# The order of the last products of a dense layer, and where its output blocks are joined to the rows

## The chip, the core and the metric

The kernel runs on one core of a Trainium2 chip. The time is device microseconds of one execution, given as the median of three runs; the profile comes from an execution of its own. Engines are named PE (TensorE, matrix products; PEld is its weight load), DVE (VectorE), ACT (ScalarE), POOL (GpSimd) and SP (SyncE, which issues DMAs). ACT can issue DMAs too.

## What is computed

A graph of 1250 nodes with 512 features and 20,000 edges passes two layers. The first is a normed neighbour mean, a linear map and kernel attention. The second is this one:

```python
h = relu(layernorm(x))
agg = segment_sum(h[src], dst, num_segments=N)
h = (1.0 + eps) * h + agg
h = relu(batch_norm(h @ W1 + b1, g1, be1))     # 512 -> 1024
h = h @ W2 + b2                                # 1024 -> 512: the second dense layer
h = relu(batch_norm(h, g2, be2))
return x + h
```

`batch_norm` takes mean and variance of each feature over all 1250 nodes, so no output of a feature can be finished before every node's sum for it is there. Adding a constant such as `b2` to a feature moves its mean and leaves its variance.

## The kernel before

**Layout.** Activations are kept transposed: features on the 128 partitions, nodes along the free dimension, padded to 1252 = 2 x 626 (`HN`). The output of the second dense layer, `o`, has four blocks f = 0 to 3 of 128 features. `xs` holds the residual rows, nodes on partitions, in ten row groups (nine of 128, the last of 98).

**Seven products.** Both dense layers use a Strassen-Winograd scheme: the weights and the activations are quartered, and seven products of quarters (numbered 1 to 7) with sums before and after take the place of eight. Class `Dense` (L749) does this for two output blocks at a time. Instance `a` has blocks 0 and 2, `b` blocks 1 and 3 (block m + 2 i). `multiply(p)` (L758) issues product p on PE into two banks of PSUM, one for each half (313 nodes, `NH`) of 626: 2 halves x 4 steps over the contraction, each an f32 matmul that the profile shows as two records, so 16 records. Products 2, 3 and 5 go to banks B, the others to banks A. Products 1, 6, 7, 4 follow each other in A without clearing it, 5 and 3 in B.

**After a product** (`after`, L792): ACT copies A aside with the bias added (`keep`, after 1, 6, 7). DVE adds such a copy to B and so writes a quarter of `o` (`join`, after 2, 7, 3), then takes statistics of the two halves (`stats`). After product 4, ACT writes the quarter (block i = 1, first 626 nodes) straight from A with the bias. With `direct`, used for the very last product, DVE takes the statistics from A in PSUM rather than from `o`, and adds the bias to the means in them (L812).

**Norm and rows.** `norm` (L816) calls `affine` (L123): aggregate four sets of statistics (`bn_aggr`), root on ACT, reciprocal and three small operations on DVE, giving `sb`, a scale and a shift for each feature. `apply` (L870) norms a block of `o` in place: nodes 0 to 511 and 1024 to 1249 on DVE, 512 to 1023 on ACT. `rows_of` (L878) turns the block back to rows with ten 128 x 128 transposes on PE into three PSUM tiles; `finish` (L886) adds max(., 0) to `xs` on DVE (two operations of 4 row groups, one of 1 group and one of 98 rows) and issues four output DMAs (256, 256, 64 and 49 KB), two on SP and two on ACT.

**Order.** The loop at L921 gives the order of the last products of `a` and `b`: a6, a5, b6, a7, b5, b7, a4 (norm of block 2), a3 (norm of block 0, then the rows of block 2), b3 (norm of block 1, then the rows of block 0), and then b4 with the statistics taken directly (L930). The rows of block 1 are transposed behind b4 and joined only among the joins of block 3 (L932 to L940). Matmuls and transposes keep the program's order on PE, and so do the marked DVE operations (`order`); each engine works in order, waiting on semaphores of the others. All eight PSUM banks belong to one pool (`mm`): four to `a`, four to `b`; a new tile takes the place of the oldest when its last reader is done.

Of the kernel before, what the change touches and what calls it, by code (L numbers as in the profile page):

```python
# [11 lines left out]
F32 = mybir.dt.float32  # L12
# [4 lines left out]
AF = mybir.ActivationFunctionType  # L17
ALU = mybir.AluOpType
# [3 lines left out]
N, D, E = 1250, 512, 20000  # L22
HID = 2 * D
KD = D // 128
KH = HID // 128
# [4 lines left out]
BSPLIT = [(0, 512), (512, 512), (1024, 226)]  # L30
# [7 lines left out]
S = 128  # L38
NJ = -(-N // S)
ROWS = [min(S, N - j * S) for j in range(NJ)]  # L40
# [14 lines left out]
HN = 626  # L55
NH = HN // 2
# [13 lines left out]
def sorted_graph(ctx: ExitStack, tc: tile.TileContext, ed, x, n1g, n1b, n2g, n2b, wconv, bconv,  # L70
                 wq, wk, wv, wo, proj, eps, w1, b1, g1, be1, w2, b2, g2, be2, out):
    nc = tc.nc
# [50 lines left out]
    def affine(sb, st, g, b, shift=None):  # L123


        mv = tmp.tile([128, 2], F32, name="mv")
        r = tmp.tile([128, 2], F32, name="r")
        nc.vector.bn_aggr(mv, st.rearrange("p i s -> p (i s)"))  # L128
        nc.scalar.activation(r[:, 0:1], mv[:, 1:2], AF.Sqrt, bias=epsc, scale=1.0)  # L129
        if shift is not None:  # L130
            nc.vector.tensor_tensor(mv[:, 0:1], mv[:, 0:1], shift, ALU.add)
        nc.vector.reciprocal(r[:, 0:1], r[:, 0:1])
        nc.vector.tensor_tensor(r[:, 1:2], r[:, 0:1], negT[:, g:g + 1], ALU.mult)
        nc.vector.tensor_tensor(sb[:, 0:1], r[:, 0:1], vT[:, g:g + 1], ALU.mult)
        nc.vector.scalar_tensor_tensor(sb[:, 1:2], mv[:, 0:1], r[:, 1:2], vT[:, b:b + 1], op0=ALU.mult, op1=ALU.add)
# [15 lines left out]
    mm = att.enter_context(tc.tile_pool(name="mm", bufs=4, space=PSUM))  # L151
# [27 lines left out]
    col, at, r = {}, {}, 0  # L179
    for name, v in vectors.items():  # L180
        k = v.shape[0] // 128
# [329 lines left out]
    for f in range(KD):  # L511
        ps = mm.tile([128, TOK], F32, name="mm")
# [18 lines left out]
    mm = ctx.enter_context(tc.tile_pool(name="mm2", bufs=8, space=PSUM, reuse_waits="tile"))  # L531
# [3 lines left out]
    xs = p2.tile([S, NJ, D], F32, name="xs")  # L535
# [29 lines left out]
    for f in range(KD):  # L565
        fs = slice(f * 128, (f + 1) * 128)
        st = tmp.tile([128, 3, 6], F32, name="st")
        for i, (n0, n) in enumerate(BSPLIT if f == KD - 1 else ESPLIT):
            c = slice(n0, n0 + n)
            ps = banks.pop(0)[:, :n] if banks else mm.tile([128, n], F32, name="mm")  # L570
# [9 lines left out]
            b = at["bconv"] + f  # L580
# [8 lines left out]
        sb = tmp.tile([128, 2], F32, name="sb")  # L589
# [86 lines left out]
    for g, after in zip(groups[2:], groups[3:] + ((),)):  # L676
        w = slice(g[0], g[-1] + 1)
        order(nc.vector.reciprocal(rs[:, w], rs[:, w]))
        order(nc.vector.scalar_tensor_tensor(nb[:, w], mv[:, w, 0], -1.0, rs[:, w], op0=ALU.mult, op1=ALU.mult))
        for j in g:  # L680
            n = ROWS[j]

            for t in (hi, h2):
                nc.scalar.activation(t[:n, j, :], xs[:n, j, :], AF.Relu, bias=nb[:n, j:j + 1], scale=rs[:n, j:j + 1])
        for j in after:
            joined(j)
            measured(j)
        if after:
            root(after)
        for j in g:  # L690
            lows(j)
# [24 lines left out]
    for t in range(6, NJ):  # L716
# [8 lines left out]
        for j in range(3 * (t - 6), min(3 * (t - 6) + 3, NJ)):  # L725
            n = ROWS[j]
# [14 lines left out]
    def add(engine, out, x, y, op):  # L741
        order(engine.tensor_tensor(out, x, y, op))
# [6 lines left out]
    class Dense:  # L749
# [42 lines left out]
        def after(self, p, direct=False):  # L792

            if p == 1:
                self.keep(1, 0)
            elif p == 2:
                self.join(0, 0, 1)
            elif p == 6:
                self.keep(6, 0)
            elif p == 7:  # L800
                self.keep(7, 1)
                self.join(1, 1, 7)
            elif p == 3:
                self.join(0, 1, 6)
            elif p == 4:
                for c in range(2):
                    o, b, st, _ = self.part(1, 0, c)
                    nc.scalar.activation(o, self.A[c], AF.Identity, bias=b, scale=1.0)
                    if direct:

                        order(nc.vector.bn_stats(st, self.A[c]))
                        order(nc.vector.tensor_scalar(st[:, 1::3], st[:, 1::3], b, None, op0=ALU.add))  # L812
                if not direct:
                    self.stats(1, 0)

        def norm(self, i, g, be):  # L816
            sb = tmp.tile([128, 2], F32, name="sb4", bufs=4)
            f = self.m + i * self.half
            affine(sb, self.st[i], at[g] + f, at[be] + f)
            return f, sb  # L820

    w2t = weight(w2, "w2", p4, "w2")
# [17 lines left out]
    for m0 in (0, 2):  # L840
        d = {c: Dense(ops1, m, KH // 2, hid, "b1") for c, m in zip("ab", (m0, m0 + 1))}
        for p, c in ((1, "a"), (2, "a"), (1, "b"), (2, "b"), (6, "a"), (6, "b"), (5, "a"), (5, "b"), (7, "a"), (7, "b"),
# [15 lines left out]
            if p == 3:  # L858
                relu(d[c], 0)
                k = d[c].m  # L860
# [9 lines left out]
    def apply(o, sb):  # L870
        for i, (n0, n) in enumerate(BSPLIT):
            c = o[:, n0:n0 + n]
            if i == 1:
                nc.scalar.activation(c, c, AF.Identity, bias=sb[:, 1:2], scale=sb[:, 0:1])
            else:
                order(nc.vector.tensor_scalar(c, c, sb[:, 0:1], sb[:, 1:2], op0=ALU.mult, op1=ALU.add))

    def rows_of(o):  # L878
        for n0, n in BSPLIT:
            j0 = n0 // S  # L880
            ps = mm.tile([S, 4, 128], F32, name="mm")
            for j in range(j0, -(-(n0 + n) // S)):
                nc.tensor.transpose(ps[:ROWS[j], j - j0, :], o[:, j * S:j * S + ROWS[j]], ident)
            yield ps

    def finish(f, sets):  # L886

        fs = slice(f * 128, (f + 1) * 128)
        for i, ((n0, n), ps) in enumerate(zip(BSPLIT, sets)):
            j0 = n0 // S  # L890
            js = range(j0, -(-(n0 + n) // S))
            whole = [j for j in js if ROWS[j] == S]
            w = slice(j0, j0 + len(whole))
            order(nc.vector.scalar_tensor_tensor(xs[:, w, fs], ps[:, :len(whole), :], 0.0, xs[:, w, fs],  # L894
                                                 op0=ALU.max, op1=ALU.add))
            queue = nc.scalar if i == 1 else nc.sync
            queue.dma_start(out[j0 * S:(j0 + len(whole)) * S, fs].rearrange("(j p) d -> p j d", p=S), xs[:, w, fs])
            for j in js:
                if j not in whole:
                    k = ROWS[j]  # L900
                    order(nc.vector.scalar_tensor_tensor(xs[:k, j, fs], ps[:k, j - j0, :], 0.0, xs[:k, j, fs],
                                                         op0=ALU.max, op1=ALU.add))
                    nc.scalar.dma_start(out[j * S:j * S + k, fs], xs[:k, j, fs])
            yield
# [13 lines left out]

    for k in range(KH // 2):
        add(nc.vector, rh[0, 1][:, k, :], rh[0, 1][:, k, :], th[:, 0, k, :], ALU.subtract)  # L920
    for d, p in ((a, 6), (a, 5), (b, 6), (a, 7), (b, 5), (b, 7), (a, 4), (a, 3), (b, 3)):  # L921
        d.multiply(p)
        d.after(p)
        if p in (3, 4):
            f, sb = d.norm(p - 3, "g2", "be2")
            apply(o[:, f], sb)
        if p == 3:
            for _ in finish(2 * (d is a), rows_of(o[:, 2 * (d is a)])):
                pass
# [12 lines left out]

@with_exitstack
# [455 lines left out]
def tile_gnn(ctx: ExitStack, tc: tile.TileContext, x, src, dst, *rest):  # L1399
# [171 lines left out]
    with tc.If(v == 0) as arms:  # L1571
        sorted_graph(tc, ed, x, *rest)
# [33 lines left out]
```

## Time and profile before

| | |
|---|---|
| time, median of 3 runs | 376.24 us (375.83 to 377.05) |
| profiled execution, its own time | 377.66 us |
| its span, first to last instruction | 375.9 us |
| PE busy | 357.0 us (95%) |
| DVE, ACT, POOL busy | 235.6, 157.4, 35.4 us |
| granted TensorE clock, mean | 0.989 |
| DMA moved | 18.06 MB |

The span is shorter than the execution's own time, because something precedes the first and follows the last instruction. Times in the profile are us from the start of the span. A timeline line gives start, duration, engine, line of the kernel, operation, what it writes and reads with shapes, how often it comes (merged neighbours), and in brackets how long the engine had been idle and who ended that. In the two lines of slices each digit is a fortieth of the span in tenths. A line of a stretch gives its bounds, length, busy time of PE, PEld, DVE, ACT and POOL with the number of instructions, the granted clock, the mean busy share of the 16 DMA engines and GB/s. A line of a source line's instructions gives how many there were, their least, median and longest duration in ns, and the first and last start.

### The profile page before, as it was taken

The page shows a single profiled execution, that of the slowest core. Times are in us where ns is not written, and L with a number is a line of the kernel's source. Part 1 is how long each engine was busy: PE and PEld are TensorE (multiplying, and loading weights), DVE is VectorE, ACT ScalarE, POOL GpSimd, SP SyncE. Part 2 cuts the span into 40 slices and gives each one's busy share as a digit, 9 for nine tenths or more (in the row PEclk, how much of TensorE's full clock was granted, in tenths as well). Part 3 has the DMA queues.
Part 4 walks back from the last instruction along what each step waited for, and adds up shares of the span by engine and source line. Part 5 has one row for each costly group of instructions (what it writes and reads, how often), then busy time and mean ns, then how long its engine had stood idle before and what let it go on. Part 6 is the DMA issues. An engine that isn't in the chain of part 4 may idle for free.

```text
span 375.9 us, 4922 instructions
## 1 busy us (share of the span) xinstructions
PE 357.0 (95%) x1840; PEld 263.3 (70%) x1840; DVE 235.6 (63%) x585; ACT 157.4 (42%) x310; POOL 35.4 (9%) x55
## 2 busy tenths in 40 slices
PE   8799989999999999999999999999999999999970
PEld 4665555676566699998768888777777777777750
DVE  6899994649897235687887232182780888212783
ACT  5498549727565360111157312232652542111230
POOL 3000000000000005000000009610062000000000
PEclk9999999999999999999999999999999999999995
DMA  6943020000000471000000000240000000000045
GB/s 200 289 166 128 16 98 0 2 1 2 0 1 2 151 279 67 0 3 0 0 2 0 2 0 1 55 171 0 2 0 1 1 2 0 1 0 2 10 126 144
DMA packets 13285, 18.06 MB, mean 48 GB/s; under 512 B 1341, under 2 KB 6658, under 8 KB 13254
## 3 DMA queue, kind: packets, MB, share of 16 engines
q1 hardware_dynamic: 10622, 16.41, 13.0%
q10 hardware_dynamic: 2632, 1.27, 1.3%
q8 instruction: 16, 0.26, 0.3%
q14 instruction: 15, 0.12, 0.1%
HBM read 15.11 MB, written 2.56 MB: 47 GB/s over the span
## 4 chain that ended last, share of the span: by engine, by line
PE 83%; DVE 11%; ACT 2%; issue 1%; DMA 1%; DVEq 0%
PE mm L764 29%; PE mm L707 12%; PE mm L575 12%; PE hw L422 10%; PE mm L245 3%; PE mm L449 2%; PE mm L521 2%; PE mm L482 2%; PE sc L267 2%; PE acc L217 2%; DVE op L206 1%; DVE xs L894 1%; PE mm L226 1%; PE mm L701 1%; DVE kmx L334 1%; PE mm L472 1%
## 5 line engine op out<-in xcount | busy, mean ns | idle before, releaser
L779 ACT ACTIVATE kept<-mm,vT 128x313 f32<-128x313 f32 x36 | 18.5, 521 | 49.6 <-PE mm L764 48.5
L422 PE MATMUL hw<-wconv,xn 128*128 128x512 f32 (+1 forms) x80 | 37.1, 605 | 0.3 <-ACT adj L220 0.3
L707 PE MATMUL mm<-hi,adj 128*128 128x512 f32 (+2 forms) x100 | 32.2, 400 | 0.5 <-DVE hi L655 0.4
L707 PE MATMUL mm<-lo,adj 128*128 128x512 f32 (+2 forms) x100 | 31.7, 395 | 0.0
L129 ACT ACTIVATE r<-mv,epsc 128x1 f32<-128x1 f32 x16 | 4.7, 292 | 52.1 <-DVE mv L128 52.1
L764 PE MATMUL mm<-hid,w 128*128 128x313 f32 x96 | 25.8, 427 | 0.0
L422 PEld LDWEIGHTS hw<-wconv,xn 128*128 128x128 f32 (+1 forms) x80 | 14.1, 188 | 16.4 <-issue 14.8
L575 PE MATMUL mm<-adj,lo 128*128 128x416 f32 (+3 forms) x120 | 25.1, 355 | 0.0
L575 PE MATMUL mm<-adj,hi 128*128 128x416 f32 (+3 forms) x120 | 25.1, 355 | 0.0
L206 DVE TENSOR_TENSOR op<-iop,prow 128x1280 f16<-128x1280 f16 (+2 forms) x27 | 20.8, 769 | 6.0 <-PE acc L217 5.6
L784 DVE TENSOR_TENSOR hid<-mm,kept 128x313 f32<-128x313 f32 x24 | 10.9, 477 | 20.4 <-ACT kept L779 16.9
L764 PEld LDWEIGHTS mm<-hid,w 128*128 128x128 f32 x96 | 18.2, 190 | 6.9
L575 PEld LDWEIGHTS mm<-adj,hi 128*128 128x128 f32 x120 | 21.9, 189 | 1.1
L575 PEld LDWEIGHTS mm<-adj,lo 128*128 128x128 f32 x120 | 21.8, 189 | 1.0
L707 PEld LDWEIGHTS mm<-hi,adj 128*128 128x128 f32 (+2 forms) x100 | 18.4, 186 | 5.8 <-DVE hi L655 1.4
L698 DVE SCALAR_TENSOR_TENSOR z<-h,e,mm 128x512 f32<-128x512 f32 (+1 forms) x10 | 7.0, 745 | 23.5 <-PE mm L707 15.7
L707 PEld LDWEIGHTS mm<-lo,adj 128*128 128x128 f32 (+2 forms) x100 | 18.5, 186 | 4.6 <-DVE lo L648 0.2
L217 PEld LDWEIGHTS <-op 128*128 128x128 f16 x250 | 13.7, 97 | 9.1 <-issue 4.7
L217 PE MATMUL acc<-ok,op 128*128 128x100 f16 x250 | 16.2, 208 | 3.4 <-DVE ok L206 2.7
L784 DVE TENSOR_TENSOR o<-mm,kept 128x313 f32<-128x313 f32 x12 | 5.7, 482 | 21.5 <-ACT kept L779 20.8
L702 ACT COPY zT<-mm 128x512 f32<-128x512 f32 (+1 forms) x10 | 5.3, 583 | 29.3 <-PE mm L701 29.3
L764 PE MATMUL mm<-tz,w 128*128 128x313 f32 x64 | 17.5, 426 | 0.0
(249 smaller groups left out, 717.0 us busy)
## 6 DMA issues: line engine op xcount, KB each, us to landing
w<-in_L_gnn_W_dram SPq DMA_DIRECT2D x2, 2048.0 KB
xs<-in_x_dram SPq DMA_DIRECT2D x1, 2304.0 KB
wk<-in_L_gnn_Wk_dram SPq DMA_DIRECT2D x1, 1024.0 KB
x<-in_x_dram SPq DMA_DIRECT2D x1, 1024.0 KB
v<-in_L_gnn_Wv_dram SPq DMA_DIRECT2D x1, 1024.0 KB
wconv<-in_L_gnn_W_conv_dram SPq DMA_DIRECT2D x1, 1024.0 KB
wk<-in_L_gnn_Wq_dram SPq DMA_DIRECT2D x1, 1024.0 KB
o<-in_L_gnn_Wo_dram SPq DMA_DIRECT2D x1, 1024.0 KB
```

Of the source, the lines that this page charges most:

```text
L206: i = nc.vector.tensor_tensor(t[:, qs], iota.unsqueeze(1).to_broadcast(shape), keys[:, bt, qs].unsqueeze(2).to_broadcast(shape), ALU.is_equal)
L217: nc.tensor.matmul(acc[:, :, q * TG:(q + 1) * TG], op[:, q, :, i], ok[:, q, :, i].rearrange("p (j t) -> p j t", t=TG), start=(q == 0 and i ...
L245: nc.tensor.matmul(ps, wt[:, k, b * 128:(b + 1) * 128], hT[:, k, :TOK], start=(k == 0), stop=(k == KD - 1))
L267: nc.tensor.matmul(ps[:, a, :M], tT[a * 64:a * 64 + 64, b, t * 128:(t + 1) * 128], projT[a * 64:a * 64 + 64, :], start=True, stop=True)
L422: nc.tensor.matmul(ps[:n], xn[:, f, :n], wct[:, f, :], start=(f == 0), stop=(f == KD - 1))
L449: nc.tensor.matmul(ps[:, i, :], kf[:, t, hd, mb * 128:(mb + 1) * 128], va[:, t, hd, :], start=(t == 0), stop=(t == NT - 1))
L482: nc.tensor.matmul(pa[:, i, :], qfTs[n][:, i, mb, :], kv[:, mb, hd, :], start=(mb == 0), stop=(mb == 1))
L575: nc.tensor.matmul(ps, part[:k, j, fs], adj[:k, j, c], start=(part is hi and j == 0), stop=(part is lo and j == NJ - 1))
L707: nc.tensor.matmul(ps[:n], adj[:k, j, t * S:t * S + n], part[:k, j, :], start=(part is hi and j == 0), stop=(part is lo and j == NJ - 1))
L764: order(nc.tensor.matmul(banks[i], left[:, k, m * 128:(m + 1) * 128], right[:, k, i * NH:(i + 1) * NH], start=(p in (1, 2, 5) and k == 0), ...
L779: nc.scalar.activation(t[:, c, :], self.A[c], AF.Identity, bias=self.part(i, 0, c)[1], scale=1.0)
L784: order(nc.vector.tensor_tensor(self.part(i, j, c)[0], self.B[c], t[:, c, :], ALU.add))
```

## The change

The ten last products come in the order a6, a5, a7, b6, a4, b5, a3, b7, b3, b4. The rows of block 2 are transposed in two parts, after b5 (row groups 0 to 7) and after a3 (groups 8 and 9); those of block 0 after b7; those of block 1 inside b4: after the first half and three of the four steps of the second half, ahead of the last step. Only block 3's rows come after b4. The PSUM tiles for this are four spare ones, in the banks of `a` as they fall free (`room`), used in turn. In the diff, `take(d, p)` is `multiply(p)` and `after(p)`, and `normed_rows(d, i)` is `norm` and `apply` of a block. All output DMAs go to SP, but for two of block 3's.

The statistics of b4's quarter are both taken from the sums in PSUM without the bias, the first half's in the course of b4. The bias is instead taken off the means of block 3's other quarter beforehand, and added back to the aggregated mean (`shift`, a parameter that `affine` had). ACT no longer writes the last 313 nodes of b4's quarter to `o`; it norms them from PSUM in one step, with a shift `end` = bias x scale + shift. DVE norms the other 313 + 624 columns of block 3.

```diff
         def after(self, p):
...
             elif p == 4:
                 for c in range(2):
-                    o, b, st, _ = self.part(1, 0, c)
-                    nc.scalar.activation(o, self.A[c], AF.Identity, bias=b, scale=1.0)
-                    if direct:
-                        order(nc.vector.bn_stats(st, self.A[c]))
-                        order(nc.vector.tensor_scalar(st[:, 1::3], st[:, 1::3], b, None, op0=ALU.add))
-                if not direct:
-                    self.stats(1, 0)
+                    self.evict(c)
+                self.stats(1, 0)
+
+        def evict(self, c):
+            o, b, _, _ = self.part(1, 0, c)
+            nc.scalar.activation(o, self.A[c], AF.Identity, bias=b, scale=1.0)
+
+        def measure(self, c):
+            order(nc.vector.bn_stats(self.part(1, 0, c)[2], self.A[c]))
...
+    spare = []
+    place = itertools.cycle(range(4))
+
+    def pieces(f, parts):
         fs = slice(f * 128, (f + 1) * 128)
-        for i, ((n0, n), ps) in enumerate(zip(BSPLIT, sets)):
+        todo = []
+        for i in parts:
+            n0, n = BSPLIT[i]
             j0 = n0 // S
             js = range(j0, -(-(n0 + n) // S))
-            whole = [j for j in js if ROWS[j] == S]
+            ps = spare[next(place)]
+            for j in js:
+                order(nc.tensor.transpose(ps[:ROWS[j], j - j0, :], o[:, f, j * S:j * S + ROWS[j]], ident))
+            todo.append((i, js, ps))
+        for i, js, ps in todo:
+            j0, whole = js[0], [j for j in js if ROWS[j] == S]
             w = slice(j0, j0 + len(whole))
             order(nc.vector.scalar_tensor_tensor(xs[:, w, fs], ps[:, :len(whole), :], 0.0, xs[:, w, fs],
                                                  op0=ALU.max, op1=ALU.add))
-            queue = nc.scalar if i == 1 else nc.sync
+            queue = nc.scalar if f == KD - 1 and i == 1 else nc.sync
...
-                    nc.scalar.dma_start(out[j * S:j * S + k, fs], xs[:k, j, fs])
+                    queue = nc.scalar if f == KD - 1 else nc.sync
+                    queue.dma_start(out[j * S:j * S + k, fs], xs[:k, j, fs])
...
-    for d, p in ((a, 6), (a, 5), (b, 6), (a, 7), (b, 5), (b, 7), (a, 4), (a, 3), (b, 3)):
-        d.multiply(p)
-        d.after(p)
-        if p in (3, 4):
-            f, sb = d.norm(p - 3, "g2", "be2")
-            apply(o[:, f], sb)
-        if p == 3:
-            for _ in finish(2 * (d is a), rows_of(o[:, 2 * (d is a)])):
-                pass
-    b.multiply(4)
-    b.after(4, direct=True)
-    tail = finish(1, list(rows_of(o[:, 1])))
-    f, sb = b.norm(1, "g2", "be2")
-    apply(o[:, f], sb)
-    next(tail)
-    last = finish(3, rows_of(o[:, 3]))
-    next(last)
-    next(last)
-    for _ in itertools.chain(tail, last):
-        pass
+    def room():
+        spare.extend(mm.tile([S, 4, 128], F32, name="mm") for _ in range(2))
+
+    for d, p in ((a, 6), (a, 5), (a, 7), (b, 6), (a, 4)):
+        take(d, p)
+    normed_rows(a, 1)
+    room()
+    take(b, 5)
+    pieces(2, (0, 1))
+    take(a, 3)
+    room()
+    normed_rows(a, 0)
+    pieces(2, (2,))
+    take(b, 7)
+    pieces(0, (0, 1, 2))
+
+    order(nc.vector.tensor_scalar(b.st[1][:, 2:, 1::3], b.st[1][:, 2:, 1::3], col["b2"][:, 3:4], None, op0=ALU.subtract))
+    take(b, 3)
+    normed_rows(b, 0)
+    b.multiply(4, halves=(0,))
+    b.evict(0)
+    b.measure(0)
+    last = KH // 2 - 1
+    b.multiply(4, range(last), (1,))
+    pieces(1, (0, 1, 2))
+    b.multiply(4, [last], (1,))
+    b.measure(1)
+    bias = col["b2"][:, 3:4]
+    f, sb = b.norm(1, "g2", "be2", bias)
+    end = tmp.tile([128, 1], F32, name="end")
+    nc.vector.scalar_tensor_tensor(end, bias, sb[:, 0:1], sb[:, 1:2], op0=ALU.mult, op1=ALU.add)
+    for n0, n in ((0, NH), (HN, N - HN)):
+        c = o[:, f, n0:n0 + n]
+        order(nc.vector.tensor_scalar(c, c, sb[:, 0:1], sb[:, 1:2], op0=ALU.mult, op1=ALU.add))
+    nc.scalar.activation(o[:, f, NH:HN], b.A[1], AF.Identity, bias=end, scale=sb[:, 0:1])
+    pieces(3, (0, 1, 2))
```

In the prediction, lines L951 and `end` are the subtraction of the bias and the new shift of this diff; all other line numbers are those of the kernel before.

More of the change, by code (lines that the diff above doesn't have):

```diff
@@ L790, in stats, with after @@
                 order(nc.vector.bn_stats(st, whole))
-        def after(self, p, direct=False):
+        def after(self, p):
             if p == 1:
@@ L806, in after, with norm @@
                 for c in range(2):
-                    o, b, st, _ = self.part(1, 0, c)
-                    nc.scalar.activation(o, self.A[c], AF.Identity, bias=b, scale=1.0)
-                    if direct:
-                        order(nc.vector.bn_stats(st, self.A[c]))
-                        order(nc.vector.tensor_scalar(st[:, 1::3], st[:, 1::3], b, None, op0=ALU.add))
-                if not direct:
-                    self.stats(1, 0)
-        def norm(self, i, g, be):
+                    self.evict(c)
[5 more added lines that the diff above has]
+            order(nc.vector.bn_stats(self.part(1, 0, c)[2], self.A[c]))
+        def norm(self, i, g, be, shift=None):
             sb = tmp.tile([128, 2], F32, name="sb4", bufs=4)
             f = self.m + i * self.half
-            affine(sb, self.st[i], at[g] + f, at[be] + f)
+            affine(sb, self.st[i], at[g] + f, at[be] + f, shift)
             return f, sb
@@ L876, in apply @@
                 order(nc.vector.tensor_scalar(c, c, sb[:, 0:1], sb[:, 1:2], op0=ALU.mult, op1=ALU.add))
[L878 to L886, printed above, removed]
+    spare = []
+    place = itertools.cycle(range(4))
+    def pieces(f, parts):
         fs = slice(f * 128, (f + 1) * 128)
-        for i, ((n0, n), ps) in enumerate(zip(BSPLIT, sets)):
+        todo = []
+        for i in parts:
+            n0, n = BSPLIT[i]
             j0 = n0 // S
             js = range(j0, -(-(n0 + n) // S))
-            whole = [j for j in js if ROWS[j] == S]
+            ps = spare[next(place)]
[4 more added lines that the diff above has]
+            j0, whole = js[0], [j for j in js if ROWS[j] == S]
             w = slice(j0, j0 + len(whole))
@@ L902, in finish @@
                                                          op0=ALU.max, op1=ALU.add))
-                    nc.scalar.dma_start(out[j * S:j * S + k, fs], xs[:k, j, fs])
-            yield
+                    queue = nc.scalar if f == KD - 1 else nc.sync
+                    queue.dma_start(out[j * S:j * S + k, fs], xs[:k, j, fs])
     o = nat.tile([128, KD, 2 * HN], F32, name="o", tag="T")
@@ L920, in sorted_graph, with take, normed_rows @@
         add(nc.vector, rh[0, 1][:, k, :], rh[0, 1][:, k, :], th[:, 0, k, :], ALU.subtract)
-    for d, p in ((a, 6), (a, 5), (b, 6), (a, 7), (b, 5), (b, 7), (a, 4), (a, 3), (b, 3)):
+    def take(d, p):
         d.multiply(p)
         d.after(p)
-        if p in (3, 4):
-            f, sb = d.norm(p - 3, "g2", "be2")
-            apply(o[:, f], sb)
-        if p == 3:
-            for _ in finish(2 * (d is a), rows_of(o[:, 2 * (d is a)])):
-                pass
-    b.multiply(4)
-    b.after(4, direct=True)
-    tail = finish(1, list(rows_of(o[:, 1])))
-    f, sb = b.norm(1, "g2", "be2")
-    apply(o[:, f], sb)
-    next(tail)
-    last = finish(3, rows_of(o[:, 3]))
-    next(last)
-    next(last)
-    for _ in itertools.chain(tail, last):
-        pass
+    def normed_rows(d, i):
+        f, sb = d.norm(i, "g2", "be2")
+        apply(o[:, f], sb)
+    def room():
[32 more added lines that the diff above has]
+    pieces(3, (0, 1, 2))
 @with_exitstack
```

## The prediction

> **What bounds the kernel now.** I read the page's slices first, then the chain that ended last, then the timeline from 343 us on, last the stretches of the tail.
>
> ```profile
> PE   8799989999999999999999999999999999999970
> DMA  6943020000000471000000000240000000000045
> ```
>
> TensorE is full until the last two slices (9.4 us each); only there do the DMA engines work again. So until its last product this stage costs its matmuls, and after that a serial tail. From the timeline:
>
> ```profile
> 351.51 1.26 PE L883 MATMUL mm<-ident,o 128*128 128x128 f32 x10
> 351.72 0.48 DVE L784 TENSOR_TENSOR o<-mm,kept 128x313 f32<-128x313 f32 x1 [0.62 <-PE mm L764]
> 354.29 0.85 DVE L876 TENSOR_SCALAR o<-o,sb 128x512 f32<-128x512 f32 x2
> ...
> 357.91 4.38 PE L764 MATMUL mm<-hid,w 128*128 128x313 f32 x16
> 362.17 0.49 ACTq L903 DMA_DIRECT2D out_dram<-xs  x1
> 362.71 0.52 ACT L808 ACTIVATE o<-mm,vT 128x313 f32<-128x313 f32 x1 [1.89 <-DVE st L812]
> 363.27 0.49 DVE L811 BATCH_NORM_STATS2 st<-mm 128x6 f32<-128x313 f32 x1 [0.56 <-ACT o L808]
> 363.79 0.23 DVE L812 TENSOR_SCALAR st<-st,vT 128x2 f32<-128x2 f32 x1
> 365.07 0.22 DVE L135 SCALAR_TENSOR_TENSOR sb<-mv,r,vT 128x1 f32<-128x1 f32 x1
> 366.02 1.28 PE L883 MATMUL mm<-ident,o 128*128 128x128 f32 x10 [2.64 <-DVE o L876]
> 366.10 2.68 DVE L894 SCALAR_TENSOR_TENSOR xs<-mm,xs 128x512 f32<-128x512 f32 x5
> 369.08 0.28 DVE L901 SCALAR_TENSOR_TENSOR xs<-mm,xs 98x128 f32<-98x128 f32 x1
> 369.21 2.18 ACTq L903 DMA_DIRECT2D out_dram<-xs  x2
> ```
>
> The last product, b4, is 16 matmul records; the last ends at 362.29. Then come statistics (ACT's eviction stands behind an output DMA that ACT was still issuing at 362.17), the norm, ten transposes at 366.02, and eight joins to xs, four for block 1 and four for block 3 (366.10 to 369.37). Both blocks' eight DMAs follow, the last one's issue ending on ACT at 369.21 + 2.18 = 371.39. Stretches:
>
> ```profile
> 363.39:366.02 2.63, 0.00 (x0) 0.03 (x1) 2.13 (x9) 0.93 (x2) 0.00 (x0) 1.00 0.38 95
> 367.30:367.90 0.60, 0.01 (x1) 0.00 (x0) 0.60 (x3) 0.00 (x0) 0.00 (x0) 0.98 0.33 94
> 367.90:372.20 4.30, 0.00 (x0) 0.00 (x0) 1.47 (x6) 0.00 (x0) 0.00 (x0) 0.50 1.05 281
> 372.20:374.20 2.00, 0.00 (x0) 0.00 (x0) 0.00 (x0) 0.00 (x0) 0.00 (x0) 0.50 0.20 42
> ```
>
> Last columns: granted clock, DMA share, GB/s. Two blocks (1.28 MB) keep the DMA engines full until 372.2; stragglers run to 374.2; 1.7 us more ends the span. A second chain ends as late, the jump past the other arm of the If:
>
> ```profile
> L1571 PEldq COMPARE_BRANCH  x2: 90/1689/3288, 10.3 to 366.6; - x2
> L1571 ACTq COMPARE_BRANCH  x2: 38/42/45, 12.7 to 371.5; - x2
> L1601 ACTq DRAIN  x2: 8/37/66, 375.0 to 375.4; - x2
> ```
>
> ACT branches at 371.5, just after its last DMA issue, and does its next thing at 375.0: 3.5 us. PE's jump took 3.29 us. Span end minus end of ACT's last issue: 375.89 - 371.39 = 4.50.
>
> **The change, step by step.** A product is 16 records at 0.2635 us start to start (357.91 to 362.13): 4.216 us. A transpose is 0.109 us.
>
> *Order of the products.* The same ten products stand on PE from 317.80, so the order by itself adds nothing if no operand is late. a4 starts at 334.66 instead of 343.09. The norm's chain after a product takes 3.63 us from PE's end to the end of the apply (a3: 351.51 to 354.29 + 0.85). Block 2 is thus ready at 338.88 + 3.4 = 342.3, before b5 ends at 343.09; its eight transposes go there. a3 ends at 348.18 and block 0 is ready at 351.8, before b7 ends at 352.61. Cover: 0.8 us each. Without it PE would wait up to 3.63 us. The accumulators: a7 and b7 wait for ACT's copies and b3 for the joins of product 7; by the same rows these are done at 352.9 for the first half, 0.8 us before b3 starts at 353.70. Net 0.
>
> *DVE's queue.* Between block 0's apply (done 351.8) and b3's end lie, in order: two joins of block 2 (0.48), two joins of product 7 (0.96, the second not before ACT's copy at 353.3), two statistics (0.86), four joins of block 0 (1.59: starts 0.60, 0.60, 0.20, 0.20 apart), and the new subtraction of the bias from two means (L951, 0.23 as L812). That ends at 356.45. The following join of b3's first half must be done when its second half ends, near 358.1: 1.2 us spare. b3 ends at 357.91 (before: 356.82, as block 0's transposes came after it), so block 1 is normed 1.09 later, DVE at 360.69 to 361.54. ACT's share starts at 360.77, since the first half of b4 is evicted ahead of it (360.22 to 360.74), and ends at 361.59.
>
> *Block 1's rows among the last matmuls.* b4 starts at 357.91 as before; 14 records end at 361.60, then ten transposes: the first wants DVE's 361.23 plus 0.15 (the gap from L876's end to L883 in the tail), so 0.2 us spare; ACT's 361.59 is wanted only at 362.04. Then b4's last two records. b4 ends 10 x 0.109 = 1.09 us later, at 363.39: this lies fully on the path. The four joins of block 1 (362.23 to 363.91) hold DVE's queue, so the last statistics start at 363.83 rather than 363.43: 0.4 us more.
>
> *Statistics and norm.* Gone from the path: ACT's late eviction (the statistics waited for it, not for PE) and both bias additions (0.26 start to start). The shift of the mean (0.16) runs beside ACT's root (0.29): nothing; were it alone, 0.16. Aggregation starts at 363.83 + 0.48 + 0.03 = 364.34, against 364.06: +0.28. The same chain gives scale and shift at 365.58. New: `end`, one column, 0.22 plus 0.03, to 365.83. ACT then norms 313 columns from the sums (0.52) until 366.42 and DVE 313 and 624 columns. From L876 (512: 0.545, 226: 0.393) these cost 0.44 and 0.60: done at 366.19 and 366.71. Bounds for reading sums instead of memory on ACT: 0.52 (L808's row, taken) and 0.81. Transposes start at 366.34 (+0.32); the fourth ends at 366.95, the eighth at 367.46.
>
> *Tail.* Only four joins remain: 366.97, 367.57, 368.17, 368.37, ending at 368.65 (before: 369.37). All DMAs of blocks 2, 0 and 1 go to SP, 12 issues of 0.35 to 0.49; block 1's start at 362.95, and its 0.64 MB need 3.5 us from the first issue to the last packet (block 0 before: first issue 361.07, quiet by 364.5), so they are gone by 366.5, when block 3's first is issued at 367.68. The DMA that waits longest for an old semaphore waits for block 0's, some 8 us earlier. ACT issues two for block 3; the last starts 0.13 after the last join (as in the case of 362.04 to 362.17), at 368.78, and takes 0.49 (0.72 after block 2; the 1.0 to 1.1 at the end came with a full queue). So 369.27.
>
> *The end, two ways.* By data: 367.68 + 3.45 = 371.13 for the last packet, plus 1.7: 372.8, i.e. -3.1. [...] ACT's row agrees that some wait of 3.5 us lies behind its branch, and it starts only after ACT's last issue. So 369.27 + 4.50 = 373.77: -2.1. I take this one; with 0.72 for the issue it is -1.9.
>
> *The clock.* [...] The row: the ten transposes after 2.63 us ran at 1.00, but the clock fell to 0.50 at 367.9, only 0.6 us behind them, although 1.28 us of work lay just before. [...]
>
> **Sum.** b4's end +1.09. From there to the aggregation 0.95 instead of 364.06 - 362.29 = 1.77: -0.82; `end` +0.25; from the scale and shift to the transposes 0.51 instead of 0.73: -0.22; from the transposes to the last join 2.31 instead of 3.35: -1.04; from the last join to the end of ACT's last issue 0.62 instead of 2.02: -1.40. Together -2.1 us. The profiled execution took 377.66, 1.8 around its span of 375.9; the median shown, 376.24, lies 1.4 below it. The difference is applied to the median: **374.1 us**.
>
> **Rivals.** *Data, not the jump, ends the span*: the jump's cost shrinks with less traffic; 373.2. For: PE's and DVE's jumps, in a quieter queue, took 3.3 and 3.2 us. Against: that is still over 3. [...] *The writes still end it*: stragglers took 2.0 us behind the saturated stretch, now too: 371.1 + 2.0 + 1.7 = 374.8, -1.1, so 375.2. Against: blocks 2 and 0 showed no such stragglers. *DVE's queue becomes the bound, slower*: in-order joins of blocks 2 and 0 push b3's join back; TensorE stands before block 1's transposes with b4's last records behind them. Beyond 1.2 + 0.2 us of backlog each us costs one; at 3.5 the gain is gone, at 4.7 it is 377.4. For: DVE is 4.1 of 4.65 us busy there. Against: that would need those rows doubled.
>
> **How the numbers follow.** 0.3% (1.13 us) is about what a measurement can tell. Forecast 0.62, its own range 373.6 to 374.6; data ends it 0.10; half clock 0.13; writes 0.10; slower 0.05. Faster: 0.62 + 0.10 + 0.07 of the half clock + 0.03 of the writes = 0.82; the rest of these two is 0.13 of no change. The range, 373.1 to 375.3, takes in the ends of the three smaller faster cases and leaves out the slower one.
>
> **What would show it.** Right: TensorE without a gap to 363.4; statistics of b4's second half at 363.8; last transposes near 366.3; last join near 368.7; ACT's last issue before 369.6; ACT's DRAIN about 3.5 us behind its branch. Wrong: PE waiting at block 1's transposes; clock 0.50 at 366.3; data still moving at 373.

## The result, and the profile after

The changed kernel takes 376.38 us (median of 22 executions, 373.82 to 377.34), against 376.97 us (375.83 to 378.96) for 22 of the kernel before on the same chip. The two medians lie 0.6 us apart. The ratio of the executions, compared round by round, is 0.9967, with a 95% interval of 0.9952 to 0.9983: 0.33% or 1.2 us faster. The forecast was 374.1 us and 2.1 us faster. So the direction was right, the size was not, and the range of 373.1 to 375.3 missed the time.

The times of the kernel before lie mostly on two levels about 2 us apart (ten of the 22 from 375.8 to 376.4, ten from 377.7 to 379.0), and those of the changed kernel are spread over 3.5 us. For this reason the steps are compared below inside the profiled executions, from the start of the first of the ten products (a6) to the end of the span. That stretch took 58.09 us before and 56.73 after: 1.35 us less.

The slices after, PE and DMA:

```profile
PE   8799989999999999999999999999999999999981
DMA  6953020000000372000000000150000000001133
```

Before, only the last two slices showed output; now the last four do, since block 2 is written from 344.5 us on, block 0 from 355.3 and block 1 from 363.0. The timeline from b4's last step on:

```profile
362.71 0.69 PE L764 MATMUL mm<-hid,w 128*128 128x313 f32 x2
363.86 0.48 DVE L816 BATCH_NORM_STATS2 st<-mm 128x6 f32<-128x313 f32 x1
365.65 0.22 DVE L965 SCALAR_TENSOR_TENSOR end<-vT,sb 128x1 f32<-128x1 f32 x1
365.91 0.61 ACT L969 ACTIVATE o<-mm,end,sb 128x313 f32<-128x313 f32 x1 [0.94 <-DVE end L965]
366.28 1.39 PE L893 MATMUL mm<-ident,o 128*128 128x128 f32 x10 [2.88 <-DVE o L968]
367.05 1.49 DVE L898 SCALAR_TENSOR_TENSOR xs<-mm,xs 128x512 f32<-128x512 f32 x3 [0.30 <-PE mm L893]
367.77 2.18 SPq L902 DMA_DIRECT2D out_dram<-xs  x2
368.41 0.45 ACTq L902 DMA_DIRECT2D out_dram<-xs  x1
368.45 0.28 DVE L906 SCALAR_TENSOR_TENSOR xs<-mm,xs 98x128 f32<-98x128 f32 x1
368.98 1.25 ACTq L909 DMA_DIRECT2D out_dram<-xs  x1
```

The last statistics start 0.45 us after b4's last record ends (363.41), the ten transposes start at 366.28, and four joins stand behind them where eight stood. The last join ends at 368.73; before, it was 369.37, with b4 ending 1.1 us earlier. All this is within 0.1 us of the forecast. The last line is not: ACT's last DMA issue takes 1.25 us. The stretches of the tail (columns as before: bounds, length, PE, PEld, DVE, ACT, POOL, clock, DMA share, GB/s):

```profile
363.41:366.28 2.87, 0.00 (x0) 0.00 (x0) 2.56 (x13) 0.67 (x2) 0.00 (x0) 1.00 0.75 223
366.28:367.68 1.40, 1.39 (x10) 1.03 (x10) 1.09 (x3) 0.24 (x1) 0.00 (x0) 1.00 0.00 0
367.90:371.10 3.20, 0.00 (x0) 0.00 (x0) 0.83 (x3) 0.00 (x0) 0.00 (x0) 0.51 0.70 200
371.10:371.90 0.80, 0.00 (x0) 0.00 (x0) 0.00 (x0) 0.00 (x0) 0.00 (x0) 0.50 0.21 61
371.90:374.55 2.65, 0.00 (x0) 0.00 (x0) 0.00 (x0) 0.00 (x0) 0.00 (x0) 0.50 0.04 9
```

Block 1's data moves while the last statistics and norm run (0.75 of the DMA engines), and is through when the transposes start (0.00). Block 3's data is through by 371.65, the last packet. So the output is through 2.9 us before the end. ACT's jump lasts longer:

```profile
L1601 ACTq COMPARE_BRANCH  x2: 38/42/45, 12.8 to 370.3; - x2
L1631 ACTq DRAIN  x2: 8/38/67, 373.7 to 374.0; - x2
L909 ACTq DMA_DIRECT2D out_dram<-xs x1: 1245/1245/1245, 369.0 to 369.0; - x1
```

ACT branches when its issue is over (370.3), and does its next thing, a DRAIN, 3.4 us later (373.7). SP, which at the end waits 2.4 us in all for output to land, passes its DRAIN at 373.0.

### The profile page after: what moved, and what is told of

Its sections match the earlier page's. It is cut to its first block, busy times and chain, and to the rows that moved or that the text cites. A ratio compares the mean times of both kernels' runs of the same rounds, so it can differ in the third digit from the quotient of the medians.

```text
span 374.5 us, 4916 instructions
## 1 busy us (share of the span) xinstructions
PE 357.0 (95%) x1840; PEld 262.8 (70%) x1840; DVE 236.2 (63%) x586; ACT 156.6 (42%) x309; POOL 35.4 (9%) x55
## 4 chain that ended last, share of the span: by engine, by line
PE 87%; DVE 9%; ACT 2%; DMA 1%; issue 1%; DVEq 0%
PE mm L764 31%; PE mm L707 12%; PE mm L575 12%; PE hw L422 10%; PE mm L245 3%; PE mm L449 2%; PE mm L521 2%; PE mm L482 2%; PE sc L267 2%; PE acc L217 2%; DVE op L206 1%; PE mm L226 1%; PE mm L701 1%; DVE kmx L334 1%; PE mm L472 1%; PE mm L893 1%
## 5 line engine op out<-in xcount | busy, mean ns | idle before, releaser
L764 PE MATMUL mm<-hid,sw 128*128 128x313 f32 x64 | 17.5, 427 | 0.0
```

The costliest lines, as they stand in the source:

```text
L764: order(nc.tensor.matmul(banks[i], left[:, k, m * 128:(m + 1) * 128], right[:, k, i * NH:(i + 1) * NH], start=(p in (1, 2, 5) and k == 0), ...
```

## The experiments

Two theories of the slow last issue on ACT were put against each other. One (F, fetch): it is slow because code for the jumps of PE and DVE, which have finished earlier, is being fetched by the same DMA engines. The other (S): SP and ACT slow each other because both issue at once. A third cause is the forecast's own, queues that are full of data. Further questions were whether the jump (theory J) or the data decides the end, and what the change's other parts are worth. "a6 to end" below is the stretch of the profiled execution named above; every ratio is to the kernel before.

### The same kernel again

No edit.

> The changed kernel once more, for its scatter and a second trace. All theories: span 374 to 375 us, the last join of block 3 near 368.7 us, and the last output issues slow again: 1.2 us on ACT, 1.4 us on SP.

Measured: 375.32 us, ratio 0.996 (0.9942 to 0.9978), a6 to end 56.94 us. The last issue on ACT took 1.79 us this time, and SP's last took 0.34 (in the first profile, 1.38). What follows: the gain repeats, the slow last issue too, but its length varies, and it isn't always both engines that are slow. S does not fit this profile: SP's last issue was over at 368.82, and ACT's slow one ran from 368.89 to 370.68.

### Without the other arm: the changed kernel, and the kernel before

```diff
-    with tc.If(v == 0) as arms:
+    with tc.If(v == 0):
...
-    with arms.Else():
-        any_graph(tc, ed, x, src, dst, *rest)
```

> The changed kernel without the arm for unsorted edges (that computation is left out; the edges of this input are sorted, so the arm never runs): the jump at the end leads nowhere far. Theory F (the code fetches of PE's and DVE's jumps hold DMA engines while the last outputs are issued): the last issues take 0.35 to 0.6 us on SP and ACT, ACT's DRAIN comes within 1 us of its branch, the last packet near 371.1, span near 372.6. Theory S (SP and ACT slow each other because both issue at once): the issues stay at 1.2 to 1.4 us, span 373 or more.

> The kernel before, also without that arm. Theory F: the last four issues take 0.35 to 0.6 us instead of 0.96 to 1.12, stragglers behind 372.2 us are gone or under 0.7 us, span near 373.9, so that between the two kernels without the arm lie 1.3 us or less. By the prediction's own two ways of counting (data ends it, -3.1; jump ends it, -2.1) the difference without the jump would be 3.1 us less its share of stragglers, about 2. Theory S: issues as in the kernel before.

Measured: the changed kernel without the arm takes 374.85 us, ratio 0.9924 (0.9902 to 0.9946), a6 to end 55.48. The kernel before without the arm takes 376.38, ratio 0.9959 (0.9941 to 0.9976), a6 to end 56.73. ACT's branch and the DRAIN behind it now stand 0.16 us apart in both. The issues of the changed kernel, from the answer on its source lines:

```profile
L909 ACTq DMA_DIRECT2D out_dram<-xs x1: 692/692/692, 367.1 to 367.1; - x1
L902 SPq DMA_DIRECT2D out_dram<-xs x11: 344/377/511, 342.6 to 366.7; - x11
```

And the timeline of the kernel before without the arm:

```profile
367.01 3.27 SPq L897 DMA_DIRECT2D out_dram<-xs  x4
369.42 1.86 ACTq L903 DMA_DIRECT2D out_dram<-xs  x2
```

What follows for the changed kernel. With no far jump, the last issue takes 0.69 us instead of 1.25 or 1.79, and SP's 0.34: F is right so far, though 0.69 is above its 0.6. The span that it expected, 54.8 us from a6 on, was missed by 0.7: without the jump the data ends this version, with the last packet at 369.61 and the end 1.80 us later.

For the kernel before, F's 0.35 to 0.6 us did not come true: the last three issues take 0.84, 0.84 and 0.93 without any fetch (with the arm: 0.97, 0.96 and 1.12). With the arm, too, no code was being fetched during these three. They ran from 369.21 to 371.39, and the DMA engines carried only this from 369.2 to 371.4 (queue and kind: packets, MB, share):

```profile
q10 hardware_dynamic: 887, 0.45, 74.3%
q1 hardware_dynamic: 398, 0.19, 32.2%
```

The two packets of code (kind "instruction") had been under way from 367.51 to 368.44 and from 368.83 to 369.14. So the slow issues of the kernel before came with a queue that holds two blocks, and the change takes that away. But it also brings the last issue forward, from 52.5 us after a6's start to 51.2, and there it meets the fetch, whose packets ended at 51.3 before and end at 51.7 now.

Leaving out the arm brings the end forward by 1.25 and 1.46 us against the two profiles of the changed kernel, and by 1.36 in the kernel before, whose last packet comes 1.67 us earlier as well. The difference between the kernels is 1.24 us without the arm and 1.35 with it, so the jump is not where the change's gain went.

### Jumps that come later

Twelve idle transposes on PE and four copies on DVE behind the last join, so that neither engine jumps while block 3's DMAs are being issued.

```diff
     pieces(3, (0, 1, 2))
+    late = mm.tile([S, 4, 128], F32, name="mm")
+    k = ROWS[NJ - 1]
+    for i in range(12):
+        order(nc.tensor.transpose(late[:, i % 4, :k], xs[:k, NJ - 1, f * 128:(f + 1) * 128], ident[:k, :k]))
+    seen = tmp.tile([128, 4], F32, name="seen")
+    for i in range(4):
+        order(nc.vector.tensor_copy(seen[:, i:i + 1], late[:, i, 0:1]))
```

> The changed kernel with 12 transposes on PE behind the last join of block 3 and 4 small copies on DVE behind those, so that both engines jump at 369 us or later and their code is fetched behind the last issues. Theory F: the last issue takes 0.45 to 0.7 us on ACT and 0.35 to 0.5 us on SP, ACT's DRAIN comes near 373.0, span 373.7 to 374.0 (0.5 to 0.8 us less than the changed kernel's 374.5), although work was added. Theory S: issues of 1.2 and 1.4 us as before, span 374.5 or more.

Measured: 377.11 us, ratio 0.9994 (0.9977 to 1.0011), a6 to end 57.70. The timeline:

```profile
367.56 2.39 PE L893 MATMUL mm<-ident,o 128*128 128x128 f32 x10 [2.87 <-DVE o L968]
370.36 0.28 DVE L906 SCALAR_TENSOR_TENSOR xs<-mm,xs 98x128 f32<-98x128 f32 x1
370.88 0.69 ACTq L909 DMA_DIRECT2D out_dram<-xs  x1
```

The last issue took 0.69 us, with the far arm in place and block 3's data in the queue as before. What differs is what the DMA engines carried during the issues. First the kinds of traffic of the changed kernel from 367.9 to 370.3, then of this one from 369.7 to 371.6:

```profile
q1 hardware_dynamic: 510, 0.25, 38.2%
q10 hardware_dynamic: 352, 0.18, 23.7%
q8 instruction: 1, 0.02, 3.2%
q14 instruction: 1, 0.01, 1.8%
```

```profile
q1 hardware_dynamic: 528, 0.26, 47.3%
q10 hardware_dynamic: 143, 0.07, 12.7%
```

The two packets of kind "instruction", 16 and 8 KB, are the only kind that the second lacks. In the changed kernel they were under way from 367.93 to 369.17 and from 368.85 to 369.55, on both sides of the start of ACT's last issue (368.98); here the first came at 372.79. So with one block queued it is the fetch that goes with the slow issue: with the same data queued and no fetch under way it takes 0.69, twice. The total expected of this run was wrong for two other reasons. The clock fell to half just at block 3's transposes (0.51 from 367.56 to 369.00, 2.39 us for the ten), and the last join came 0.63 us later after b4 than in the changed kernel; and PE's and DVE's own jumps, started late, now ended last: PE branched at 370.9 and went on at 375.4, DVE at 373.1 and 376.0.

### All of block 3's DMAs on SP

```diff
-            queue = nc.scalar if f == KD - 1 and i == 1 else nc.sync
+            queue = nc.sync
...
-                    queue = nc.scalar if f == KD - 1 else nc.sync
+                    queue = nc.sync
```

> The changed kernel with block 3's two DMAs on ACT moved to SP: ACT issues none at the end and jumps at 366 to 367 us, so its code fetch runs beside the last joins. Theory F with J (ACT's jump behind its slow last issue sets the end): the end is set by the last data instead; ACT's DRAIN near 370, SP's last issue ends between 369.9 (quick) and 370.7 us (slow as ACT's was), the span is 1.1 to 0.5 us under the changed kernel's when both are counted from the start of a6 (56.7): 55.6 to 56.2. Rival: data, not the jump, sets the end of the changed kernel: no gain, 56.7, or more for the serial issues.

Measured: 376.08 us, ratio 0.9963 (0.9945 to 0.9981), a6 to end 56.89. ACT's jump starts at 366.4, its DRAIN comes at 369.2, long before the end. SP, which issues all four, branches at 371.3 and passes its DRAIN at 374.3. The last line is from the answer on SP's waits (line, what for: us in total, times, longest):

```profile
L1601 SPq COMPARE_BRANCH  x2: 43/46/49, 8.6 to 371.3; - x2
L1631 SPq DRAIN  x3: 7/7/7, 374.3 to 374.7; - x3
SPq L1631 <- DMA out_dram<-xs: 2.4, 3, 1.7
```

These 3 us are not a jump. SP's first instruction behind the branch starts 0.2 us after it, at 371.48, and 2.4 us of the rest is spent waiting for output that has not landed. So the data ends this version: its last packet is at 373.32, 55.04 us after a6's start, against 53.84 in the changed kernel. With four issues behind each other in one queue the last one starts 52.1 us after a6, not 51.2, and a fetch was under way among the last packets (371.9 to 372.9). The expected 55.6 to 56.2 us was missed, since it priced the slow last issue but not the later data. That the data sets the end of the changed kernel itself does not follow: there ACT's DRAIN came 0.7 us behind SP's.

### Only the last DMA moved to SP

The second of the two edits above alone: ACT issues one of block 3's DMAs (256 KB), SP three.

> Only block 3's last DMA (49 KB) moved from ACT to SP; ACT keeps the 256 KB one. Theory J: ACT's last issue ends near 368.9, its DRAIN comes near 372.3, span from a6's start 55.5 to 56.2 (changed kernel 56.7). Rival (data sets the end): 56.7.

> The variant with one DMA on ACT at the end, once more beside it. Theory J: ACT's last issue is done before 369.3 and its DRAIN comes about 3.4 us later, before SP has seen the last output land; span from a6's start 55.9 to 56.4, against 56.7 and 56.9 of the changed kernel; ratio to the kernel before 0.9945 to 0.9965. Rival: within the scatter of the changed kernel, 56.7 or more.

Measured twice: 375.62 us, ratio 0.9967 (0.9945 to 0.9989), a6 to end 56.13; and 375.21, ratio 0.9943 (0.9922 to 0.9965), a6 to end 55.66. Expected were 55.5 to 56.2 and 55.9 to 56.4. In the first, ACT's last issue ends at 369.20 and its DRAIN comes at 372.67; SP's last two issues took 0.72 and 0.56, and its DRAIN comes last, at 373.47, after 2.5 us of waiting for output (last packet at 372.19). In the second, ACT's DRAIN (372.48) and SP's (372.60, last packet at 371.59) come almost together, so that jump and data end it at the same time. The last issues of the second:

```profile
368.37 0.44 ACTq L902 DMA_DIRECT2D out_dram<-xs  x1
369.00 1.44 SPq L909 DMA_DIRECT2D out_dram<-xs  x1
```

The slow issue (with the same two instruction packets under way) is now SP's. In the profiles this version ends 0.6 to 1.3 us earlier than the changed kernel, counted from a6. The ratios cannot tell it from the changed kernel (0.9967 and 0.996), since the intervals overlap.

### Block 1's rows behind b4

The rows of block 1 are transposed after b4 and joined among block 3's, as before the change; the rest of the change stays.

```diff
-    b.multiply(4, range(last), (1,))
-    pieces(1, (0, 1, 2))
-    b.multiply(4, [last], (1,))
+    b.multiply(4, range(last + 1), (1,))
     b.measure(1)
+    one = turn(1, [spare[next(place)] for _ in range(3)])
...
-    pieces(3, (0, 1, 2))
+    three = turn(3, [spare[next(place)]] + [mm.tile([S, 4, 128], F32, name="mm") for _ in range(2)])
+    for block, todo in ((1, one[:1]), (3, three[:2]), (1, one[1:]), (3, three[2:])):
+        add_in(block, todo)
```

(`turn` and `add_in` are the two halves of `pieces`, transposes and joins.)

> One part undone: block 1's ten transposes behind b4 and its joins among block 3's, as in the kernel before; all else as changed (its DMAs on SP). By the prediction's steps: b4 ends 1.1 us earlier, last transposes near 364.8, eight joins from 365.2 to 368.5, 0.3 us before the changed kernel's; but 1.28 MB are then issued from 365.9 on, full rate to 370.6, stragglers to 371 to 372.6; span from a6's start 56.5 to 57.5 against 56.7. So this part alone is worth between -0.2 and +0.8 us. If the part carried the whole gain, as the sum has it (-1.0 for joins, -1.4 for issues, +1.1 for the transposes and +0.4 for the statistics), 57.6 or more.

Measured: 376.33 us, ratio 0.999 (0.9965 to 1.0015), a6 to end 57.30, within the expected 56.5 to 57.5 and 0.57 and 0.36 more than the two profiles of the changed kernel.

```profile
365.12 1.39 PE L893 MATMUL mm<-ident,o 128*128 128x128 f32 x10 [1.38 <-DVE o L971]
365.49 2.68 DVE L902 SCALAR_TENSOR_TENSOR xs<-mm,xs 128x512 f32<-128x512 f32 x5
368.48 0.28 DVE L910 SCALAR_TENSOR_TENSOR xs<-mm,xs 98x128 f32<-98x128 f32 x1
371.15 1.32 SPq L906 DMA_DIRECT2D out_dram<-xs  x1
```

b4 ends 1.09 us earlier after a6 (44.50 against 45.59), the last join 0.31 earlier (50.61 against 50.92): on the engines alone this is the shorter way. It loses at the queues: eight DMAs are to be issued at the end, six of them on SP (before the change four on each queue, which this run does not restore), and the last issue (on SP) ends at 372.47, 54.3 us after a6, against 52.4 for the changed kernel's; the last packet is at 373.67. So this part of the change costs 0.3 us on the engines and, by the profiles, gains 0.4 to 0.6 in all; as far as this run shows, what it gains lies in the output that is out of the way. The interval of the ratio does not separate this from the changed kernel.

### Statistics and norm as before

ACT writes b4's second half to `o`, the bias is added to b4's means, and the norm reads `o`; the order of products and rows stays.

```diff
-    order(nc.vector.tensor_scalar(b.st[1][:, 2:, 1::3], b.st[1][:, 2:, 1::3], col["b2"][:, 3:4], None, op0=ALU.subtract))
...
         def measure(self, c):
-            order(nc.vector.bn_stats(self.part(1, 0, c)[2], self.A[c]))
+            _, b, st, _ = self.part(1, 0, c)
+            order(nc.vector.bn_stats(st, self.A[c]))
+            order(nc.vector.tensor_scalar(st[:, 1::3], st[:, 1::3], b, None, op0=ALU.add))
...
+    b.evict(1)
     b.measure(1)
-    bias = col["b2"][:, 3:4]
-    f, sb = b.norm(1, "g2", "be2", bias)
...
+    normed_rows(b, 1)
```

> One part undone: the last quarter is evicted by ACT, its statistics wait for that and get the bias added, and the norm reads memory as in the kernel before; all else as changed. By the prediction's steps: aggregation 0.4 us later, no step for the end shift (0.25 less), apply and first transposes as before: last transposes 0.45 us later, last join 0.3 to 0.4 us later, span the same 0.3 to 0.4 us over the changed kernel's (57.1 from a6's start). Rival: the end shift eats the gain, 0.1 us or less.

Measured: 375.84 us, ratio 0.9984 (0.9963 to 1.0006), a6 to end 57.31, 0.58 and 0.37 more than the two profiles of the changed kernel (expected: 0.3 to 0.4).

```profile
363.08 0.26 DVE L128 BATCH_NORM_AGGREGATE mv<-st 128x2 f32<-128x24 f32 x1
364.96 1.31 PE L895 MATMUL mm<-ident,o 128*128 128x128 f32 x10 [3.26 <-DVE o L880]
```

The aggregation comes 0.40 us later after a6 than in the changed kernel, PE waits 3.26 us for the transposes instead of 2.88 (0.38 more), and the last join comes 0.30 later. This part is worth 0.3 to 0.4 us on the engines, as expected. The interval of the ratio does not separate it from the changed kernel. ACT's last issue took 1.10 us here, again with both packets of code under way (366.39 to 368.18).

### The last DMA on SP, and PE kept busier at the start

The version above, and two more idle matmuls at the kernel's start (eight instead of six), so that PE is busier there. The question is whether full clock is then granted earlier.

```diff
-        keep_up(6)
+        keep_up(8)
```

> The variant with one DMA on ACT at the end, and 8 instead of 6 idle matmuls on PE at its start (1.2 us on), which fill the half microsecond in which PE waits before its first product of work. Theory C (the two levels of the times, 1.9 us apart, come from when TensorE's clock is granted in full: at 4.2 to 5.1 us or at 9.5 to 10.4 us): more runs at the lower level, median 1 to 1.5 us under the same variant without them; a6 starts at 316.0 to 316.4. Rival (the levels come from elsewhere): no shift, or 0.3 us slower for the later first product.

Measured: 374.50 us (seven executions, 373.50 to 375.32), ratio 0.9927 (0.9901 to 0.9953), a6 to end 56.29 us; full clock is granted at 6.48 us of the span instead of 9.5 (before), and a6 starts at 316.43 instead of 317.80. This is the lowest ratio of the kernels with both arms. Its lead over the kernel before is beyond doubt; over the changed kernel (0.9952 to 0.9983 and 0.9942 to 0.9978) and over the same version with six idle matmuls (0.9922 to 0.9965) it is not, since the intervals overlap. The median is 0.7 us under that version's, not the expected 1 to 1.5. One profile can't show that the two matmuls brought the early grant, since two kernels with six had it too (below). It would be better still but for this:

```profile
362.02:364.88 2.86, 0.00 (x1) 0.00 (x0) 2.55 (x13) 0.66 (x2) 0.00 (x0) 1.00 0.74 224
364.89:367.14 2.25, 2.25 (x10) 1.97 (x10) 1.39 (x3) 0.24 (x1) 0.00 (x0) 0.50 0.03 7
```

The ten transposes run at half clock (0.50) after a gap as long as in the changed kernel (2.86 against 2.87 us): 2.25 us instead of 1.39, and the last join 0.64 later. The three executions with this profile's mean clock (0.989) took 374.50 to 374.68, the three with 0.992 or 0.993 only 373.50 to 374.25, which fits such a loss. The last three issues took 0.45, 0.34 and 0.44 us, and no packet of code was under way: PE had jumped earlier (365.6), 2 us ahead of ACT's issue.

## Why the prediction was right and wrong

**The engines' part was right, term by term.** PE has no gap until b4 ends at 363.41 (forecast 363.39: block 1's transposes cost 1.09 us). The aggregation starts at 364.38 (364.34), `end` is done at 365.87 (365.83), the last transposes start at 366.28 (366.34), the last join ends at 368.73 (368.65). From b4's end to the last join the kernel took 7.08 us before and 5.33 after; -1.75 with +1.11 of b4's shift leaves -0.64, against -0.72 forecast. ACT's norm from PSUM took 0.61 us, between the bounds of 0.52 and 0.81; DVE's second apply ends after it (366.74 against 366.52), and the ten transposes took 1.39 us instead of 1.28, so at most 0.1 was waited for. The undoing of single parts bears the signs out: 0.3 to 0.4 us for statistics and norm, and the rows of block 1 a loss on the engines and a gain in the output.

**The step that failed** is the last term of the sum, "from the last join to the end of ACT's last issue 0.62 instead of 2.02: -1.40". It rested on "takes 0.49 (0.72 after block 2; the 1.0 to 1.1 at the end came with a full queue)". The issue took 1.25 us (1.79 in the second profile), and started 0.12 later after the join than reckoned, behind ACT's previous issue. The term was 370.22 - 368.73 = 1.49, so -0.53 instead of -1.40. This is 0.87 us, and with the last join 0.08 late it makes the 0.95 by which the issue ends late (370.22 instead of 369.27). The wait behind it was 4.32 us instead of 4.50, giving 0.18 back: the span ended at 374.55 instead of 373.77, 0.78 late.

**Why it failed.** The forecast put the 1.0 to 1.1 us of the last issues before down to a full queue, and that holds for the kernel before: without any fetch these issues still take 0.84 to 0.93, and with the arm no fetch was under way beside them. What it left out is that the last issue, once it comes earlier, meets the code fetches of PE and DVE. The trace of the kernel before shows them: PE and DVE branch at 366.6 and 367.5, and the packets of kind "instruction" (16 and 8 KB) start at 367.51 and 368.83; in the changed kernel the branches are at 367.0 and 367.8 and the packets start at 367.93 and 368.85; without the arm there are none in this stretch (366 to 368 changed, 366 to 371.4 before). The forecast priced a jump as a wait of the engine that jumps, 3.5 us for ACT, and not as traffic that other engines' issues meet. That the last issue is slow with the fetch and quick without it is shown by taking the fetch away (0.69) and by putting it off (0.69), and in act_one_warm it was over in time (0.44, on SP); with it the issue took 1.25, 1.79 and 1.10, and 1.44 on SP. Each of these is one profile. In what way the fetch does it is not shown: with one under way SP's issues took anything from 0.34 to 1.44, and the last one in the run with all issues on SP 0.38. And not all of the miss is the fetch: of the 0.76 us by which the issue was longer than 0.49, 0.20 is there without one. 0.69 is near the forecast's alternative of 0.72, with which it would have said -1.9.

**The rivals.** *Data ends the span* fell for the changed kernel: the last packet was at 371.65 (forecast 371.13) and 1.7 behind it is 373.35, 1.2 before the end. It is the next bound, though: where ACT's jump is out of the way (one_arm_after, all on SP, one run of the last DMA on SP), the data ends the span. In the kernel before, the two were level: SP's wait for the output ended at 375.07, ACT's jump at 375.00. *Half clock*, 0.13 of the chances: no run shows a length of gap that brings it. It did not occur at the last transposes in the profiles of the changed kernel, after gaps of 2.88 and 2.87 us, but did in two of the variants (0.51 in late_jumps, 0.50 in act_one_warm), both after 2.87, where the last join came 0.63 and 0.64 us later. *The writes still end it* fell, as few packets were left behind 371.1 (shares of 0.21, then 0.04). *DVE's queue as the bound* fell: b4 ends where the count of matmuls puts it.

**The median.** It misses 374.1 by 2.3 us, of which the failed step is 0.8. Another 0.7 is the base: the change was subtracted from 376.24, the median of three, while the 22 executions of the kernel before have 376.97. The last 0.8 is that the two medians lie only 0.6 us apart, where the profiles show 1.35 and the ratio 1.2; with times that are spread over 3 us and more, neither median is a firm figure.

## What to carry to other kernels

When a tail is shortened, look at what other engines start when they finish early: here the engines that were done jumped, and their code fetches ran through the DMA engines (367.93 to 369.55) just as the last output was issued (367.77 to 370.22). A duration that is read from a crowded stretch can have more than one cause (here 0.84 to 0.93 us with two blocks queued and no fetch, 1.10 to 1.79 on ACT with one block and a fetch), so before it is dropped from a sum, ask which of them the change takes away. In the profiles here, moving output ahead of the last product paid although it cost the engines 0.3 us, since issues queue one behind the other at the end (the last one ended 54.3 us after a6 with block 1's rows behind b4, 52.4 without), and both the jump of the engine that issues last and the landing of its data come behind the last of them (DRAIN at 373.7 and last packet at 371.65 against 370.22 in the changed kernel). When one of several ends that lie close together is moved, look which is next: here it was the data, less than 1 us behind the jump.

## What the runs showed of the hardware that was not expected

**The clock is granted on a grid.** In nine of the twelve profiled executions full clock stays granted for 358.40 us in one piece; in one_arm_after and sums_undone it is 361.81, 3.41 us more; in late_jumps 348.16, after a half-clock stretch of 3.413 us at the start. All are whole numbers of 3.413 us (105, 106, 102). The length of the gap ahead of the last transposes does not alone decide whether they run at half clock: one of 2.86 or 2.87 us had no effect in the changed kernel (the clock fell at 367.94, behind the transposes) and cost 0.64 us in act_one_warm (it fell at 364.88). Estimated from the matmul records, the 3.41 us at whose end the clock fell had PE busy for 0.16 of them in act_one_warm and late_jumps and for 0.35 to 0.41 in the other ten, and the 3.41 us ahead of these, which kept full clock, for 0.47 or more. So here the clock fell though PE had not been idle throughout; no limit can be read from this, as 3.41 us at the start of late_jumps lost it at 0.61.

**When full clock is first granted moves all that follows.** Where it was granted at 4.2, 5.1 or 6.5 us of the span (one_arm_after, sums_undone, act_one_warm), a6 started at 315.9, 316.1 and 316.4; where at 9.4 to 10.4, at 317.7 to 318.3; and in late_jumps, with the grant at 9.2 and the half-clock stretch from 16.0 to 19.4, at 319.1. Two groups of 20 matmuls near the start show the clock itself. In the kernel before the first runs ahead of the grant and the second behind it; in sums_undone and act_one_warm the first already runs behind it (timelines of PE, in this order):

```profile
7.50 2.21 PE L1528 MATMUL keys<-pick,ks 124*128 124x125 f16 x20
9.55 1.29 PE L1528 MATMUL keys<-pick,kd 124*128 124x125 f16 x20
```

```profile
6.76 1.29 PE L1553 MATMUL keys<-pick,ks 124*128 124x125 f16 x20
```

```profile
7.08 1.30 PE L1558 MATMUL keys<-pick,ks 124*128 124x125 f16 x20
```

This lies 300 us ahead of the change and is as large as it, which is why the steps are compared from a6 on. Whether this is what spreads the times of one kernel is not shown: each run has one profile, and the other executions have none.

**A jump past the other arm costs PE, ACT and DVE about 3 us each.** In the runs with both arms PE's took 3.3 to 3.8 us (4.5 in late_jumps), ACT's 2.7 to 4.3 and DVE's 2.8 to 3.4. Without the arm they take 0.18, 0.16 and 0.22. Leaving the arm out was worth 1.25 to 1.46 us of the end in either kernel, as much as the whole change.

**SP's end is the landing of the output.** Its DRAIN stands 0.7 to 1.6 us behind the last packet of output in all twelve runs, with the arm or without it (0.99 and 0.72), so its 3.0 us from branch to DRAIN in the run with all issues on SP is no price of a jump.
